# A scan, attention and expert kernel on one core: expert sums moved to SBUF, lane copies ahead of the exponentials, weighted sums behind the scores

## The chip, the cores and the metric

The kernel runs on one core of a Trainium2 chip. The metric is the device time of one execution in microseconds. The core has five engines with a queue each: TensorE (PE, whose weight loads are listed apart as PEld), VectorE (DVE), ScalarE (ACT), GpSimd (POOL) and SyncE (SP), which issues all the transfers that matter here. Each engine works its queue off in the order in which the program put it there.

## The reference

Two layers on an input of shape (4, 128, 64, 64): four images, 128 channels, 4096 positions each. All data are float32.

```
# layer 0
x = x + conv(group_norm(x))      # layer norm, depthwise 3x3, layer norm, gelu, 128x128, residual,
                                 # layer norm, then a selective scan on 4 chunks of 32 channels:
    h = dA_t * h + dBu_t         #   64 inner channels, 16 states each, over all 4096 positions
    y = einsum('bdn,bn->bd', h, C_t)
                                 # gate by silu(z), out_proj, skip, layer norm, proj_w
# layer 1, on tokens t (4, 4096, 128)
t = t + attention(layer_norm(t)) # 4 heads of 32, softmax(q k / sqrt(128)) v, W_proj
router_probs = softmax(n @ router_w + router_b)          # n = layer_norm(t), 8 experts
top_p, top_i = top_k(router_probs, 2); top_p = top_p / sum(top_p)
t = t + sum_k top_p[k] * (n @ expert_w[top_i[k]] + expert_b[top_i[k]])
```

## The kernel before

**Blocks, units, slots.** An image is cut into 8 blocks of 512 positions. A *unit* is one block, one half of the scan's channels (`p`) and one of the 16 states (`n`): 4 x 8 x 2 x 16 = 1024 units. The main loop (`while slot < len(units) ...`) runs in *slots*. Each slot does one unit of the scan: `fetched` brings the broadcast rows of B and C from DRAM (three slots ahead), `decayed` has ScalarE compute `da = exp(delta * a)` (one slot ahead), and `scan` gives VectorE three instructions of 128x512: `h = rows * du`, the scan itself, and `hc = rows * h`. ScalarE copies the last column of `h` into `states` at the top of the next slot. The sixteen `hc` of a block and half are added up by TensorE, as products with the identity into the bank `y`. For image 0 every `hc` goes to TensorE by itself; from image 1 on GpSimd first adds the even and the odd one (`even`), and TensorE gets half as many.

**Attention.** Beside the scan, each slot also does one *group* of attention once its quarter of the image is ready: `attention` is a generator that issues four matmuls of scores (`sc`, key side 128 rows, queries 512 columns, two banks at a time) and two exponentials (`pT`, 128x1024) on ScalarE. `weighted` issues the eight matmuls `av` of the group of the slot before; the two query blocks `u` use the two column halves of the array. When a part ends, `avs` is copied from PSUM, added to what an earlier part left (`prev`), and sent to DRAM. There are 1024 groups; attention of image b overlaps the scan of image b + 1, and the last image's attention has the core nearly to itself.

**Lanes.** Everything else is written as generators that are stepped in two *lanes*, X and Y, each with one PSUM bank (`work("X")`, `work("Y")`) and four temporaries. `advance(lane, second)` takes a lane one `yield` further. Each slot steps a lane twice: half A issues mostly TensorE work, half B mostly the VectorE, ScalarE or GpSimd work that reads it. Lane Y runs `group_norm`, `first_norm`, `conv` and `inputs` (in-projection, Silu, B and C, softplus); lane X runs `closed` (the end of layer 0, then keys, queries and values), `divided` (divides the attention sums) and `finished` (output projection, router, top-2, experts). `normalised` is the layer norm used in all of them: VectorE's statistics, four small GpSimd instructions (`rs`, `shift`), then four ScalarE instructions `xt`.

The order within a slot before is: transfers, `states` copy, `da`; scores and exponentials of this slot's group; X's half B if its last yield was `"short"`; scan; X's half B otherwise; Y's half A; `y` products that are due; Y's half B; `weighted` of the last group; X's half A. All queue orders follow from this, since the wrappers (`Queue`, line 445) record every instruction in program order; this is why the profile gives line 445 for nearly everything.

**Experts before.** In `finished`, for each of the 4 tiles of 128 tokens and each half of the experts, one matmul of 128x512 fills the X bank with four experts' outputs, tokens on partitions, and VectorE adds them to `acc` with four `scalar_tensor_tensor` of 128x128, weighted by `pr`. These 16 steps per block yield `"short"`, so that two fit in a slot. `divided` loads the four heads' sums (`avl`), transposes them, and multiplies by reciprocals; `finished` transposes the result back (`aT`).

**Transfers.** `send` collects stores, and `flush` issues them all at the top of the next slot on SP, ahead of the fetches of rows.

Of the kernel before, what the change touches and what calls it, by code (L numbers as in the profile page):

```python
# [17 lines left out]
P = 128  # L18
C = 128
# [17 lines left out]
def conv_mamba_attn_moe_kernel(ctx: ExitStack, tc: tile.TileContext, t: dict):  # L37
# [423 lines left out]
    def send(out, in_):  # L461
        outgoing.append((out, in_))

    def flush():
        for o, i in outgoing:
            sync.dma_start(out=o, in_=i)
        outgoing.clear()
# [32 lines left out]
    def normalised(lane, src):  # L500
# [15 lines left out]
        yield  # L516
# [9 lines left out]

    group_of, y0_of, xn_of, pairs_of, in_of, gated, kqv = {}, {}, {}, {}, {}, {}, {}
# [147 lines left out]
    def inputs(b, i, p):  # L675

        xn, pairs = xn_of[b, i], pairs_of[b, i]
        r = slice(DI * p, DI * p + DI)
        ps = work("Y")
# [15 lines left out]
        bc = mix.tile([DI, BLK], F32, name="bc")  # L695
        scalar.copy(bc, pb[0:DI, :])
        bcd = dram.tile([2, NST, 2 * BLK], F32, name="bcd", bufs=4)
        send(bcd.rearrange("c n (k q) -> (c n k) q", k=2), bc)
# [62 lines left out]
    def closed(b, i):  # L761
# [20 lines left out]
        summed(ps, [(wout[:, p, :], gated.pop((b, i, p))) for p in range(2)])  # L782
# [3 lines left out]
        yield  # L786
        ps = transposed("X", by_tile(cm))
        yield
        xt = yield from normalised("X", by_tile(ps))
        ps = transposed("X", xt)  # L790
        yield
# [9 lines left out]
        send(tsave[b][:, s], tt.rearrange("p j c -> p (j c)"))  # L801
# [4 lines left out]
        send(td[:, s], tr.rearrange("p j c -> p (j c)"))  # L806
        ps = transposed("X", xt)
        yield
# [3 lines left out]
        split = []  # L812
        for d, w, bias in ((kd, wkn, bkn), (qd, wqn, bqn)):
            ps = work("X")
            mm(ps, w, xa)
            yield
            full = side.tile([P, BLK], F32, name="full")
            scalar.activation(full, ps, AF.Identity, bias=bias)
            hi = side.tile([P, BLK], F32R, name="hi", bufs=2)
            scalar.activation(hi, ps, AF.Identity, bias=bias)  # L820
            yield

            split.append((d, full, hi))
            lower(split.pop(), sj)
# [9 lines left out]

    def lower(what, s):
        d, full, hi = what
        lo = side.tile([P, BLK], F32R, name="lo", bufs=2)
        vector.tensor_sub(lo, full, hi.bitcast(F32))
        for half, w in enumerate((hi, lo)):
            w = w.bitcast(F32)  # L840
            if len(d.shape) == 4:
                send(d[:, :, half, s], w[:, None, :].to_broadcast([P, 2, BLK]))
            else:
                send(d[:, half, s], w)
# [96 lines left out]
    sums, partial, ao_of = [None], {}, {}  # L941

    def weighted(group):
# [10 lines left out]
        if last:  # L954
# [5 lines left out]
            d = dram.tile([P, BLK], F32, name=f"avd{q}{h}")  # L960
            send(d, avs)
            partial[b, q, h] = d
            if final and h == NH - 1:
                lanes["X"].append((("div", b, q), divided(b, q), []))
                for u in range(2):
                    i = 2 * q + u
                    lanes["X"].append((
                        ("out", b, i), lambda lane, b=b, i=i: finished(b, i, lane),
                        [("div", b, q)],
                    ))  # L970

    def divided(b, q):

        ao = att.tile([P, 2, NT, NH, DH], F32, name="ao", bufs=2)
        ao_of[b, q] = ao

        def load(h):
            w = att.tile([P, BLK], F32, name="avl", bufs=2)
            sync.dma_start(out=w, in_=partial.pop((b, q, h)))
            return w  # L980

        ahead = load(0)
        yield
        yield
        for h in range(NH):
            now = ahead
            if h + 1 < NH:
                ahead = load(h + 1)
            ps = transposed("X", by_tile(now))
# [188 lines left out]
    while slot < len(units) or due or waiting or left or lanes["X"] or running:  # L1178
# [47 lines left out]
        if more:  # L1226
            advance("X", True)
# [117 lines left out]
```

## Time and profile before

| what | us |
|---|---|
| median of 3 runs (lowest, highest) | 5848.51 (5847.83, 5851.88) |
| the profiled execution | 5853.82 |
| its span, first to last instruction | 5852.1 |
| mean granted TensorE clock | 0.94 |

The first page of the profile gives each engine's busy time and groups instructions by what they write and read. A group's line has the count, the busy time, the mean of one in ns, and then the idle time of the engine just before these instructions with what ended it. A stretch's line has the time, then busy time and count of PE, PEld, DVE, ACT and (where it worked) POOL, the granted clock, the share of the 16 DMA engines in use, and GB/s. A line of waits says who waited for whose work: total us, times, longest. Matmuls overlap, and one of a group can show more time than it keeps the array.

### The profile page before, as it was taken

The numbers are of one execution on the slowest core, as the hardware profiler recorded it, in microseconds if no ns is written. First come the engines' busy times: TensorE is split into PE (matmuls) and PEld (weight loads), VectorE is DVE, ScalarE is ACT, GpSimd is POOL, SyncE is SP. The second block draws the span as 40 slices with busy tenths as digits, with TensorE's granted clock in tenths as the row PEclk, the third lists the DMA queues.
The fourth block names the chain that finished last, engine by engine and source line by source line (L and its number), as shares of the span: only waits on it lengthen the run. The fifth ranks groups of instructions, "written<-read, shape, count | busy, mean of one in ns | idle before, by whom it ended". The sixth has DMA issues, their size and how long they took to land. (4 is left out here: it accounts for less than half of the span.)

```text
span 5852.1 us, 61426 instructions
## 1 busy us (share of the span) xinstructions
PE 5075.6 (87%) x18378; PEld 2129.7 (36%) x18378; DVE 4221.9 (72%) x7155; ACT 3988.0 (68%) x6116; POOL 2033.6 (35%) x1821
## 2 busy tenths in 40 slices
PE   4676898988989898898999998898999998998896
PEld 2222343333333333333333333333333343343332
DVE  4888766778877787787888887888888888712222
ACT  3454676877767776777777776677877777665452
POOL 2333222335423443444443443444443434310000
PEclk8777999999999998999999999999999999999997
DMA  3455565556545555556555555457555555533211
GB/s 98 167 177 169 196 203 182 190 209 223 202 149 172 198 186 197 172 198 219 185 199 199 188 199 191 155 196 252 191 192 199 183 201 185 190 134 102 99 58 35
DMA packets 405509, 1030.33 MB, mean 176 GB/s; under 512 B 42785, under 2 KB 126130, under 8 KB 405170
## 3 DMA queue, kind: packets, MB, share of 16 engines
q1 hardware_dynamic: 404002, 1025.53, 51.5%
q8 instruction: 149, 2.44, 0.2%
q14 instruction: 190, 1.56, 0.1%
q10 hardware_dynamic: 1168, 0.80, 0.1%
HBM read 875.11 MB, written 134.22 MB: 172 GB/s over the span
## 5 line engine op out<-in xcount | busy, mean ns | idle before, releaser
L445 ACT ACTIVATE pT<-sc 128x1024 f32<-128x1024 f32 x2048 | 1981.1, 1020 | 879.0 <-PE sc L445 875.5
L445 PE MATMUL av<-pT,v 128*64 128x512 f32 x8192 | 2012.4, 612 | 0.5 <-ACT avs L445 0.2
L445 DVE TENSOR_TENSOR_SCAN h<-da,state,h 128x512 f32<-128x512 f32 x896 | 1271.6, 1419 | 276.2 <-ACT da L445 191.5
L445 PE MATMUL sc<-qs,ks 128*128 128x512 f32 x4096 | 1326.7, 445 | 76.7 <-ACT pT L445 40.3
L445 POOL TENSOR_TENSOR hc<-hc 128x512 f32<-128x512 f32 x384 | 557.4, 1452 | 1541.4 <-DVE hc L445 1367.3
L445 PEld LDWEIGHTS sc<-qs,ks 128*128 128x128 f32 x4096 | 724.5, 193 | 663.0 <-issue 240.9
L445 PEld LDWEIGHTS av<-pT,v 128*64 128x64 f32 x8192 | 503.9, 138 | 1198.3 <-issue 1115.1
L445 DVE TENSOR_TENSOR hc<-rows,h 128x512 f32<-128x512 f32 x1024 | 828.2, 809 | 73.6 <-DVE h L445 2.3
L445 DVE TENSOR_TENSOR h<-rows,du 128x512 f32<-128x512 f32 x1024 | 821.7, 802 | 57.3 <-DMA rows<-bcd 30.9
L445 PE MATMUL y<-hc,ident 128*128 128x512 f32 x1280 | 734.3, 660 | 79.6 <-DVE hc L445 70.0
L445 ACT ACTIVATE da<-delta,amat 128x512 f32<-128x512 f32 x1024 | 749.7, 732 | 30.9 <-DVE h L445 28.7
L445 ACT COPY state<-h 128x1 f32<-128x1 f32 x896 | 176.8, 197 | 373.3 <-DVE h L445 373.0
L445 DVE SCALAR_TENSOR_TENSOR acc<-ps_X,prX,acc 128x128 f32<-128x128 f32 x864 | 301.8, 349 | 169.6 <-PE ps_X L445 145.3
L445 ACT ACT_TABLE_LOAD x318 | 408.0, 1283 | 20.0 <-PE ps_Y L445 15.3
L445 PE MATMUL ps_X<-w_ew,xf 128*128 128x512 f32 x432 | 257.2, 679 | 112.4 <-DVE acc L445 112.2
L445 PEld LDWEIGHTS y<-hc,ident 128*128 128x128 f32 x1280 | 248.7, 206 | 257.1 <-DVE hc L445 129.6
L445 DVE RECIPROCAL rden<-ps_X 128x8 f32<-128x8 f32 x64 | 13.0, 203 | 348.8 <-PE ps_X L445 348.6
L445 POOL TENSOR_SCALAR rsX<-mvX 128x4 f32<-128x4 f32 x92 | 48.3, 525 | 600.6 <-DVE mvX L445 593.6
L445 POOL TENSOR_SCALAR du<-e 128x512 f32<-128x512 f32 x64 | 129.3, 2020 | 322.3 <-ACT e L445 322.3
L445 POOL TENSOR_TENSOR avs<-avs,prev 128x512 f32<-128x512 f32 x64 | 94.6, 1478 | 420.4 <-ACT avs L445 345.8
L445 POOL TENSOR_SCALAR rsY<-mvY 128x4 f32<-128x4 f32 x100 | 54.9, 549 | 533.6 <-DVE mvY L445 532.0
L445 ACT ACTIVATE xt<-ps_Y,shiftY,rsY 128x128 f32<-128x128 f32 x380 | 143.5, 467 | 127.4 <-POOL shiftY L445 119.9
(244 smaller groups left out, 5052.1 us busy)
## 6 DMA issues: line engine op xcount, KB each, us to landing
rows<-bcd SPq DMA_DIRECT2D x1024, 512.0 KB, 4.9
ks<-kd SPq DMA_DIRECT2D x256, 512.0 KB, 6.3
qs<-qd SPq DMA_DIRECT2D x130, 512.0 KB, 5.6
v<-vd SPq DMA_DIRECT2D x256, 256.0 KB, 6.2
avd<-avs SPq DMA_DIRECT2D x128, 256.0 KB, 2.0
pairs<-xn SPq DMA_DIRECT2D x128, 128.5 KB, 2.4
qd<-hi SPq DMA_DIRECT2D x32, 512.0 KB, 5.6
qd<-lo SPq DMA_DIRECT2D x32, 512.0 KB, 5.9
```

The source lines that it names most:

```text
L445: return lambda *args, **kw: queued(op(*args, **kw))
```

## The change

In words, in the order of the diff:

- `send` takes a number of slots, and `flush` holds a store back that long. Stores of B and C rows, `tt`, `tr` and the result wait 2 slots, attention sums 3.
- `held` keeps `inputs` and the first normalisation of `closed` from using the X bank at once.
- `"early"` replaces `"short"`: where a lane X generator yields it, its next half B (ScalarE copies and activations: `xt`, `f`, `xa`, `xf`, the router's exponential, `prT`, `res`) is issued ahead of this slot's scores and exponentials instead of behind the scan.
- The out-projection `wout` is issued as two matmuls with 64 output rows each, one per half.
- The low part `lo` of keys and queries is computed from PSUM by one VectorE instruction; ScalarE's `full` goes.
- `divided` goes. Final attention sums are stored to `total` with rows in the order of the heads; `inverted` loads the denominators as 128x32, takes reciprocals, stores `inverse`; `finished` loads the sums and the reciprocals and multiplies.
- The router's probabilities are no longer divided by their sum (the top-2 weights are normalised later anyway).
- Experts: the weights of the 8 experts go to DRAM (`shares`), come back broadcast over partitions two experts at a time (`share`), VectorE multiplies them into `xf` (128x1024), and two matmuls with the experts' weights as stationary operand give the sum of two experts, which VectorE adds to `res`.
- `weighted` of the last group is issued right behind this slot's scores.
- GpSimd's pairwise sums begin at slot 128 (`ALONE`) rather than at image 1 (slot 256).
- The order of lane Y's tasks at an image's start changes, and blocks wait for `freed` instead of `closed`.

```diff
-    def send(out, in_):
-        outgoing.append((out, in_))
+    def send(out, in_, slots=1):
+        outgoing.append([slots, out, in_])
     def flush():
+        for entry in outgoing:
+            entry[0] -= 1
+            if entry[0] == 0:
+                sync.dma_start(out=entry[1], in_=entry[2])
...
@@ normalised
         yield
-        yield
+        yield "early"
         xt = tmp(lane, "xt", [P, NT, C])
...
@@ inputs
+        while held:
+            yield
+            yield
+        held.add("in")
...
@@ closed
-        summed(ps, [(wout[:, p, :], gated.pop((b, i, p))) for p in range(2)])
+        for p in range(2):
+            r = slice(DI * p, DI * p + DI)
+            mm(ps[r, :], wout[:, p, r], gated.pop((b, i, p)))
+        done.add(("freed", b, i))
...
-            full = side.tile([P, BLK], F32, name="full")
-            scalar.activation(full, ps, AF.Identity, bias=bias)
             hi = side.tile([P, BLK], F32R, name="hi", bufs=2)
             scalar.activation(hi, ps, AF.Identity, bias=bias)
+            lo = side.tile([P, BLK], F32R, name="lo", bufs=2)
+            vector.scalar_tensor_tensor(
+                lo, ps, bias, hi.bitcast(F32), ALU.add, ALU.subtract
+            )
...
@@ weighted, after the last group of a head
+            d = total[b, q]
+            send(d[:, :, h].rearrange("u k r q -> (u k) r q"), avs, 3)
+            if h == NH - 1:
+                work_left = inverted(b, q)
+                later.extend((slot + n, work_left) for n in (4, 6, 8))
+
+    def inverted(b, q):
+        den = small.tile([P, 2 * NH * BLK // P], F32, name="den", bufs=1)
+        n = den.shape[1]
+        for u in range(2):
+            sync.dma_start(
+                out=den[DI * u : DI * u + DI, :],
+                in_=total[b, q][u, 1, :, 0].rearrange("h (a n) -> h a n", n=n),
+            )
+        yield
+        vector.reciprocal(den, den)
+        inverse[b, q] = d = dram.tile([2, NH, BLK], F32, name="inverse")
+        send(d.rearrange("u h (a n) -> (u h a) n", n=n), den)
+        yield
...
@@ finished
+        sync.dma_start(out=aT, in_=total[b, q][u, 0].rearrange("h d q -> (h d) q"))
+        sync.dma_start(
+            out=inv, in_=inverse[b, q][u][:, None, :].to_broadcast([NH, DH, BLK])
+        )
...
+        vector.tensor_mul(aT, aT, inv)
...
-        for j in range(NT):
-            for u in range(2):
-                ps = work(lane, [P, NE // 2, C])
-                mm(
-                    ps.rearrange("p e c -> p (e c)"), xf[:, j * P : (j + 1) * P],
-                    ewf[:, u * BLK : (u + 1) * BLK],
-                )
-                yield "short"
-                for e in range(NE // 2):
-                    k = NE // 2 * u + e
-                    vector.scalar_tensor_tensor(
-                        acc[:, j, :], ps[:, e, :], pr[:, j, k : k + 1], acc[:, j, :],
-                        ALU.mult, ALU.add,
-                    )
...
+        shares = dram.tile([NE, BLK], F32, name=f"shares{lane}")
+        send(shares, prT)
...
+        def share(e):
...
+            sync.dma_start(
+                out=w.rearrange("p k q -> p (k q)"),
+                in_=shares[e : e + 2].rearrange("e q -> (e q)")[None].to_broadcast([P, 2 * BLK]),
+            )
+            return w
...
+        ahead = deque(share(e) for e in (0, 2))
+        yield
+        yield
+        for e in range(0, NE, 2):
+            if e + 4 < NE:
+                ahead.append(share(e + 4))
+            yield
+            w = ahead.popleft()
+            if e:
+                vector.tensor_add(res, res, ps)
+            vector.tensor_mul(w, w, xf[:, None, :].to_broadcast([P, 2, BLK]))
+            yield
+            ps = work(lane)
+            for u in range(2):
+                mm(ps, ew[:, e + u, :], w[:, u, :], u == 0, u == 1)
...
@@ the main loop
+        taken = early["X"] and advance("X", True)
         group = next(groups, None)
-        taken = short["X"] and advance("X", True)
+        if waiting:
+            weighted(waiting)
+        waiting = group
         if slot < len(units):
...
-            if b == 0:
+            if slot < ALONE:
                 due.append((slot + 1, unit, hc, n == 0))
...
         advance("Y", True)
-        if more:
-            advance("X", True)
-        if waiting:
-            weighted(waiting)
-        waiting = group
         advance("X", False)
+        while later and later[0][0] <= slot:
+            next(later.popleft()[1])
         slot += 1
```

## The prediction

> **What bounds the kernel now.** I read the first page, then the stretches, then the waits inside the long stretch, then one slot in order of time. The page first: shares of the engines and the groups that the change touches (columns: count, busy us, mean ns of one, idle of the engine before it and who ended it).
>
> ```profile
> PE 5075.6 (87%) x18378; PEld 2129.7 (36%) x18378; DVE 4221.9 (72%) x7155; ACT 3988.0 (68%) x6116; POOL 2033.6 (35%) x1821
> ...
> L445 ACT ACTIVATE pT<-sc 128x1024 f32<-128x1024 f32 x2048 | 1981.1, 1020 | 879.0 <-PE sc L445 875.5
> L445 PE MATMUL av<-pT,v 128*64 128x512 f32 x8192 | 2012.4, 612 | 0.5 <-ACT avs L445 0.2
> ...
> L445 POOL TENSOR_TENSOR hc<-hc 128x512 f32<-128x512 f32 x384 | 557.4, 1452 | 1541.4 <-DVE hc L445 1367.3
> ...
> L445 DVE SCALAR_TENSOR_TENSOR acc<-ps_X,prX,acc 128x128 f32<-128x128 f32 x864 | 301.8, 349 | 169.6 <-PE ps_X L445 145.3
> ```
>
> No engine is full: TensorE leads, yet ScalarE waits 875 us for scores and VectorE 145 us for expert products. The table of stretches (busy us of each engine, granted clock, DMA share) separates the stages: scan alone, first attention, scan and attention, attention alone, the end.
>
> ```profile
> 100.00:600.00 500.00, 331.44 (x692) 125.74 (x692) 422.29 (x587) 255.31 (x495) 164.34 (x150) 0.75 0.50 168
> 600.00:1100.00 500.00, 459.99 (x1610) 190.88 (x1608) 346.49 (x499) 361.22 (x563) 140.65 (x131) 0.96 0.57 194
> 1100.00:5110.00 4010.00, 3600.61 (x13454) 1519.56 (x13454) 3252.50 (x5315) 2988.26 (x4587) 1663.86 (x1427) 0.96 0.57 194
> 5110.00:5750.00 640.00, 588.35 (x2384) 249.08 (x2386) 141.34 (x502) 350.70 (x416) 41.19 (x56) 0.99 0.28 94
> 5750.00:5852.00 102.00, 55.35 (x130) 25.43 (x126) 35.96 (x134) 8.89 (x19) 3.40 (x8) 0.57 0.06 22
> ```
>
> In the 4010 us that decide, TensorE is 90% busy, VectorE 81%, ScalarE 75%. Three in-order queues that near one another lose time by handing over, and the waits from 600 to 5110 us name the hand-overs.
>
> ```profile
> ACT pT L445 <- PE sc L445: 607.2, 470, 8.5
> DVE acc L445 <- PE ps_X L445: 134.3, 51, 5.5
> PE ps_X L445 <- DVE acc L445: 73.7, 65, 4.8
> PE ps_X L445 <- ACT xt L445: 56.5, 46, 4.9
> ACT xin L445 <- PE ps_Y L445: 49.8, 12, 9.1
> PE ps_X L445 <- DMA avl<-avd: 39.1, 13, 8.2
> DVE stY L445 <- PE ps_Y L445: 33.5, 25, 6.4
> ```
>
> VectorE and TensorE wait for each other over one expert bank. The next rows are one lane normalisation: its shift is ready on GpSimd, ScalarE does the two exponentials first, then xt, and TensorE's transposes (and the next scores behind them) wait.
>
> ```profile
> 3222.22 1.94 ACT L445 ACTIVATE pT<-sc 128x1024 f32<-128x1024 f32 x2 [1.21 <-PE sc L445]
> 3222.67 0.24 POOL L445 TENSOR_SCALAR shiftX<-shiftX 128x4 f32<-128x4 f32 x1
> 3224.05 1.51 ACT L445 ACTIVATE xt<-ps_X,shiftX,rsX 128x128 f32<-128x128 f32 x4
> 3225.61 0.66 PE L445 MATMUL ps_X<-ident,xt 128*128 128x128 f32 x4 [0.72 <-ACT xt L445]
> ```
>
> **What the Trainium skill says.** (1) "Perfetto Trace Analysis", section "Tensor Engine Instruction (MATMUL, LD_WEIGHTS)": ACT, DVE and GpSimd are strict FIFO and a matmul's end is modelled. The trace agrees: eight av, 0.6 us each, fill 1.94 us, so 90% busy is not full. (2) "SBUF — State Buffer", section "SBUF: two separate sides": a DVE instruction with two SBUF inputs and a GpSimd instruction lock each other out. Here hc took 0.69 us alone and 1.52 beside GpSimd. The removed expert updates read PSUM (349 ns, up to 354 at most), the new products read SBUF twice. (3) "VectorE: DVE Perf Modes", section "Mode 1× (REGULAR)": one result a cycle; it prices the new product below. (4) "TensorE: Matmul & The Clock Gate", section "Part 3: Packing small matmuls": column groups of the array work side by side. The av halves do so here.
>
> **The change part by part.** Counts are from the two built orders, which take 1205 slots before and 1203 after, with 1024 scan slots and 1024 attention groups in both; so the time per slot decides. "Mixed" is 600 to 5110 us.
>
> *Experts.* Out: 1024 updates on VectorE. In: 128 products of 128x1024 and 128 additions from PSUM; matmuls stay at 256 of 128x512. Mixed: 728 updates x 0.349 = 254 us, and 147 us of VectorE idle before them, 401 us for 22.75 blocks, 17.6 each. A product: 512 elements take 0.69 us, the page's cycle adds 512/0.96 = 0.53, so 1.22 (estimate); times 0.81/0.69 (mean of hc over hc alone) 1.43. Four are 5.7, four additions at 0.686 (row tt from ps_X) 2.7, and 0.5 us wait each, 2: 10.4. So 7.2 x 22.75 = 164 us of VectorE's time, plus 3 softmax steps of 0.2 to 0.4 us a block, 17. VectorE is 80% busy and its relief partly meets the other queues: I take 110 of 181; bounds 0 and 181.
> Their cover: each pair of shares goes through DRAM. The write lands in about 2 us, the read of 512 KB like rows<-bcd in 4.9, fetched two slots (some 10 us) ahead. Without that cover VectorE would stand before the product with the next scan behind it; 128 x 2 us = 256. The 64 MB are 6% more traffic on DMA at 57%, so I take 0. The share reads join SP's one queue ahead of rows fetches; a blocked one delays rows, which are three slots ahead.
>
> *Division.* Out: per two blocks 4 x (0.203 + 0.424) on VectorE, 24 transposes on TensorE, the avl waits (39 us). In: a product of 0.7 per block, a reciprocal, two DRAM round trips started 4 to 8 slots after the sums. Net -30; bounds 0 and -75.
>
> *ScalarE.* 56 "full" x 0.70 and 23 aT x 0.59 go: 53 us. It idles 607 us for scores, so -25; bounds 0 and -53. The new lo reads PSUM at about the same 0.7.
>
> *Even lanes.* For slots 128 to 255, 64 y products of two matmuls go: 0.95 us from start to start, 61 us on a TensorE that is 92% busy from 600 to 1100. GpSimd gains 64 x 1.45 = 93 us at 28% busy and may lock VectorE (69%). -35; bounds -61 and +30.
>
> *wout* in 64-column halves, side by side: 32 x 0.8 = 26 us of TensorE, -12; bounds 0 and -26.
>
> *Early copies.* f, xa, xf, the router's exponential, prT and res (some 150 in the mixed stage) go ahead of 1.94 us of exponentials. TensorE's idle for exactly these is 36 us by group. Queued behind each are the exponentials, so the next scores: 0.2 to 0.6 us. xt (78): in the slot shown the shift is ready at 3222.91, so xt would end at 3224.4 instead of 3225.6, but the exponentials start 2.2 us later; the next scores, which had to wait for the transposes until 3226.0, can start at about 3225.4, and the exponentials after them no earlier. A wash. Net 0; bounds -93 (36 and xt's 56) and +170 (78 x 2.2).
>
> *Weighted sums behind the scores.* The eight av hold TensorE 1.87 us and pass the Y lane and y. Less: waits of ps_Y and y products, 18 + 29 + 19 + 11 = 77 us by group. More: ScalarE in the 108 input stages (Silu; Abs, Exp, Ln) waits for matmuls now behind av. There the exponentials (about 1.8 us past the scores) cover most of 1.87 but not the 0.9 to 2.6 us of matmuls: up to 1.4 x 108 = 150. Freed earlier by res, the X bank gives some back (12.6 us before w_wbc). Net 0; bounds -77 and +150.
>
> *Attention alone*, 640 us: VectorE is 22% busy and hides the products; the experts' bank wait goes (136.5 us in all, less 73.7 mixed and about 35 in the end: 28) and divisions: -35. *End*, 102 us: experts alternate bank by bank from 5785 to 5841, 56 us; two blocks x 8 matmul pairs x 2.05 at half clock are 33, plus about 6 on VectorE: -17. Division -5, two more DRAM bounces at 3.3 us +7: -15. The scan-only head keeps its work: 0. *Delayed sends* cost nothing, as their readers are 4 slots or more later.
>
> Sum: -110 - 30 - 25 - 35 - 12 + 0 + 0 - 35 - 15 = -262. The profiled execution took 5853.8, its span 5852.1; the median of the runs is 5848.5. 5848.5 - 262 = 5587, taken as 5590.
>
> **The rivals.**
> *ScalarE late, slower.* xt stands in front of the exponentials until GpSimd is done, and input matmuls stand behind av. All 78 x 2.2 + 150 = 322 us come through: 5848 - 262 + 322 = 5908. It decides once four fifths of that lateness reaches the end. For: the slot shown; ScalarE's chain in input stages. Against: TensorE's waits at the same places shrink.
> *Relief without effect.* VectorE and ScalarE get work off, but slots stay set by hand-overs; only y, wout, attention alone and the end pay: 97 us, 5751. For: three engines share the stage.
> *Hand-overs come free.* All 93 + 77 us of TensorE's lane waits go as well: 5590 - 170 = 5420. For: ScalarE's 607 us. Against: bounds of both edits have two signs.
>
> **How the numbers follow.** About 0.2% (12 us) is what a measurement can tell from no change. Forecast 0.49 (its own range 5500 to 5690), relief without effect 0.20, hand-overs free 0.11, cancelled within 12 us 0.03, slower 0.17. Faster is 0.49 + 0.20 + 0.11 = 0.80. The range from 5420 to 5880 leaves out half of the freest case and about 0.1 of the slower one.
>
> **What would show it.** Right: in the mixed stage VectorE's wait for expert products falls from 134 us to under 40, share products near 1.4 us, the slot with experts no longer above its neighbours; attention alone about 600 us; the end under 95. Wrong: a new wait of xt for shiftX above 150 us, xin and e waiting for ps_Y above 150, products near 2 us beside GpSimd, or VectorE waiting for share by DMA.

## The result: slower by 1%

| | us |
|---|---|
| before, median of 4 runs (lowest, highest) | 5849.78 (5847.83, 5851.88) |
| after, median of 4 runs (lowest, highest) | 5907.88 (5903.34, 5919.31) |
| after / before, with 95% interval | 1.0102 (1.0085 to 1.0120) |
| span of the profiled execution, before and after | 5852.1, 5901.6 |
| mean granted TensorE clock, before and after | 0.940, 0.922 |

The forecast was 5590, and the range ended at 5880. The change costs 58 us instead of saving 260.

The first page of the kernel after: shares of the engines, then groups (count, busy us, mean ns of one, idle of the engine before it and who ended most of it).

```profile
PE 5080.1 (86%) x17866; PEld 2069.8 (35%) x17866; DVE 4123.8 (70%) x6211; ACT 3932.9 (67%) x6020; POOL 2141.3 (36%) x1885
...
L445 ACT ACTIVATE pT<-sc 128x1024 f32<-128x1024 f32 x2048 | 1983.3, 1023 | 820.1 <-PE sc L445 818.1
L445 PE MATMUL av<-pT,v 128*64 128x512 f32 x8192 | 2090.9, 633 | 0.0
...
L445 POOL TENSOR_TENSOR hc<-hc 128x512 f32<-128x512 f32 x448 | 663.2, 1481 | 1651.5 <-DVE hc L445 1479.8
...
L445 DVE TENSOR_TENSOR share<-share,xf 128x1024 f32<-128x1024 f32 x128 | 174.4, 1363 | 43.3 <-DMA share<-sharesY 30.3
```

VectorE has 98 us less to do than before (4123.8 against 4221.9), ScalarE 55 us less (3932.9 against 3988.0), TensorE 512 matmuls less. The work that was to go is gone; the time is not. The table of stretches after (busy us of PE, PEld, DVE, ACT, POOL, granted clock, DMA share, GB/s) shows it in the long stretch.

```profile
100.00:600.00 500.00, 329.23 (x684) 124.37 (x682) 421.61 (x585) 249.94 (x481) 164.61 (x151) 0.75 0.50 168
600.00:1100.00 500.00, 439.12 (x1514) 177.71 (x1516) 375.69 (x501) 362.72 (x567) 218.27 (x185) 0.92 0.58 195
1100.00:5110.00 4010.00, 3547.89 (x12752) 1445.09 (x12749) 3068.37 (x4520) 2857.34 (x4405) 1647.73 (x1404) 0.94 0.60 200
5110.00:5750.00 640.00, 607.33 (x2387) 253.43 (x2385) 208.84 (x412) 381.49 (x463) 88.15 (x89) 0.98 0.47 155
5750.00:5852.00 102.00, 81.71 (x330) 32.45 (x328) 1.72 (x4) 51.57 (x54) 0.00 (x0) 0.91 0.18 54
```

From 1100 to 5110 us every one of the three engines is less busy than before (PE 3548 against 3601, VectorE 3068 against 3252, ScalarE 2857 against 2988), and the clock is 0.94 against 0.96. Three engines wait more, so something makes them wait for one another. The fourth row is busier than before only because the scan now runs on into it.

Stretches at fixed times mix stages once the kernels drift apart, so from here on I cut each trace at the first and the last of its own scans (VectorE's `h <- da, state, h`) and at the last exponentials. In us:

| stage | before | after | difference | predicted |
|---|---|---|---|---|
| slots 0 to 127, scan only | 577.6 | 579.3 | +2 | 0 |
| slots 128 to 255, even lanes new | 602.8 | 602.4 | 0 | -35 |
| slots 256 to 1022, all together | 3937.0 | 4084.6 | +148 | -177 |
| attention alone | 630.8 | 560.3 | -70 | -35 |
| end | 103.9 | 75.0 | -29 | -15 |

(The 177 are experts 110, division 30, ScalarE 25 and `wout` 12.) The two last stages give twice what was predicted, in part because work moved ahead of them: by the last scan 24 of the 32 blocks of experts are done, 23 before. The stages with a scan in every slot lose what they were to gain. These are the waits of the kernel after from 600 to 5000 us, a stretch that lies inside the scan in all the kernels (who waited for whom: total us, times, longest).

```profile
ACT pT L445 <- PE sc L445: 563.3, 361, 6.5
DVE h L445 <- ACT da L445: 340.3, 118, 8.4
...
ACT xt L445 <- POOL shiftX L445: 186.4, 58, 5.6
...
PE sc L445 <- ACT pT L445: 153.3, 189, 3.4
...
ACT xt L445 <- POOL shiftY L445: 119.7, 63, 4.6
DVE stY L445 <- PE ps_Y L445: 102.2, 50, 7.5
...
DVE xin L445 <- PE y L445: 92.6, 34, 5.4
```

The same waits before:

```profile
DVE h L445 <- ACT da L445: 196.8, 76, 21.5
...
ACT xt L445 <- POOL shiftY L445: 46.9, 32, 4.5
...
PE sc L445 <- ACT pT L445: 40.3, 63, 4.6
...
ACT xt L445 <- POOL shiftX L445: 37.6, 18, 5.6
DVE xin L445 <- PE y L445: 37.0, 20, 4.5
...
DVE stY L445 <- PE ps_Y L445: 33.5, 25, 6.4
```

Two families have grown: ScalarE at `xt` of lane X, which is an early copy, and everything that follows lane Y's matmuls. The scan's own wait, `h` for `da`, grew most, by 143.5 us; the runs below divide it up. Two places in order of time (start, duration, engine, operation, in brackets the idle time before it and who ended it) show one of each. First lane Y:

```profile
3278.95 1.94 PE L445 MATMUL av<-pT,v 128*64 128x512 f32 x8
...
3280.82 0.66 PE L445 MATMUL ps_Y<-ident,gn 128*128 128x128 f32 x4
...
3281.51 0.89 DVE L445 BATCH_NORM_STATS2 stY<-ps_Y 128x6 f32<-128x128 f32 x4 [1.95 <-PE ps_Y L445]
...
3282.77 0.57 POOL L445 TENSOR_SCALAR rsY<-mvY 128x4 f32<-128x4 f32 x1 [8.14 <-DVE mvY L445]
...
3286.76 1.51 ACT L445 ACTIVATE xt<-ps_Y,shiftY,rsY 128x128 f32<-128x128 f32 x4 [2.79 <-POOL shiftY L445]
```

The transposes into `ps_Y` start when the eight `av` ahead of them have gone in, 1.87 us after these started. VectorE, whose next instruction reads `ps_Y`, stands for 1.95 us; everything from the statistics to `xt` is late by as much, and ScalarE then stands for 2.79. Next lane X:

```profile
3300.66 1.12 PE L445 MATMUL y<-hc,ident 128*128 128x512 f32 x2
...
3303.25 0.24 POOL L445 TENSOR_SCALAR shiftX<-shiftX 128x4 f32<-128x4 f32 x1
...
3303.52 1.51 ACT L445 ACTIVATE xt<-ps_X,shiftX,rsX 128x128 f32<-128x128 f32 x4 [4.73 <-POOL shiftX L445]
...
3304.91 1.95 ACT L445 ACTIVATE pT<-sc 128x1024 f32<-128x1024 f32 x2
3305.08 1.11 PE L445 MATMUL ps_X<-ident,xt 128*128 128x128 f32 x4 [3.30 <-ACT xt L445]
3306.00 2.13 PE L445 MATMUL sc<-qs,ks 128*128 128x512 f32 x4
```

ScalarE stands 4.73 us for GpSimd with the exponentials queued behind `xt`. TensorE gets nothing for 3.30 us, and its next four scores take 2.13 us, where four took 1.17 at 3281.23. The next eight `av` take 3.46 us instead of 1.94. That is the half clock: the trace's clock record is at 0.5 from 3304.35 to 3311.17. The Trainium skill ("TensorE: Matmul & The Clock Gate", section "Part 1: The HAM clock gate (the "warmup" mystery)") says that the array drops to half rate after an idle window of about 3.4 us. Here the record drops when TensorE, by the modelled end of its last matmul, has been idle for 2.6 us; the last section counts such spells. Between 600 us and the last scan the clock records of before show 325 us at the lower level, those of after 567.

### The profile page after: what moved, and what is told of

Read it like the earlier page. It is cut to its first block, busy times and chain, and to the rows that moved or that the text cites. A ratio compares the mean times of both kernels' runs of the same rounds, so it can differ in the third digit from the quotient of the medians.

```text
span 5901.6 us, 59661 instructions
## 1 busy us (share of the span) xinstructions
PE 5080.1 (86%) x17866; PEld 2069.8 (35%) x17866; DVE 4123.8 (70%) x6211; ACT 3932.9 (67%) x6020; POOL 2141.3 (36%) x1885
## 4 chain that ended last, share of the span: by engine, by line
PE 36%; DVE 22%; ACT 14%; POOL 5%; issue 3%; DMA 3%; SPq 0%; DVEq 0%; ACTq 0%; POOLq 0%
PE av L445 15%; DVE h L445 10%; PE sc L445 9%; PE ps_X L445 6%; ACT pT L445 4%; PE ps_Y L445 3%; DVE hc L445 3%; ACT L445 3%; DVE cm L445 3%; PE y L445 3%; POOL rsX L445 2%; ACT xt L445 2%; DMA inv<-inverse 2%; DVE share L445 1%; ACT da L445 1%
## 5 line engine op out<-in xcount | busy, mean ns | idle before, releaser
L445 PE MATMUL av<-pT,v 128*64 128x512 f32 x8192 | 2090.9, 633 | 0.0
L445 PE MATMUL sc<-qs,ks 128*128 128x512 f32 x4096 | 1444.5, 472 | 189.5 <-ACT pT L445 159.8
L445 POOL TENSOR_TENSOR hc<-hc 128x512 f32<-128x512 f32 x448 | 663.2, 1481 | 1651.5 <-DVE hc L445 1479.8
L445 DVE TENSOR_TENSOR h<-rows,du 128x512 f32<-128x512 f32 x1024 | 847.8, 828 | 42.8 <-POOL du L445 29.3
L445 PE MATMUL y<-hc,ident 128*128 128x512 f32 x1152 | 687.2, 683 | 68.5 <-DVE hc L445 64.9
L445 ACT ACT_TABLE_LOAD x318 | 408.0, 1283 | 80.1 <-PE ps_Y L445 75.8
L445 PEld LDWEIGHTS y<-hc,ident 128*128 128x128 f32 x1152 | 197.9, 206 | 468.0 <-issue 221.0
L445 ACT ACTIVATE xt<-ps_Y,shiftY,rsY 128x128 f32<-128x128 f32 x380 | 143.5, 462 | 203.5 <-POOL shiftY L445 192.7
L445 PE MATMUL ps_X<-share,w_ew 128*128 128x512 f32 x448 | 221.1, 616 | 26.6 <-DVE share L445 21.3
L445 DVE TENSOR_TENSOR_SCAN h<-da,h 128x512 f32<-128x512 f32 x128 | 176.2, 1376 | 62.1 <-ACT da L445 52.0
L445 DVE TENSOR_TENSOR share<-share,xf 128x1024 f32<-128x1024 f32 x128 | 174.4, 1363 | 43.3 <-DMA share<-sharesY 30.3
L445 PE MATMUL ps_X<-ident,xt 128*128 128x128 f32 x372 | 91.8, 332 | 130.5 <-ACT xt L445 100.4
```

The source lines that it names most:

```text
L445: return lambda *args, **kw: queued(op(*args, **kw))
```

## The experiments

Four accounts were open: the weighted sums stand at the wrong place; the early copies do; ScalarE's and VectorE's new low part `lo` is late; or the planned savings were never there. All ratios are to the kernel before, with 95% intervals; sizes are differences of medians. The medians of the kernel before, taken beside each of them, lie between 5849.8 and 5858.9 us, so a difference between two runs that were not made together can be off by some 10 us.

### The two moves undone, apart and together

`weighted` back at its old place, between lane Y's half B and lane X's half A:

```diff
         group = next(groups, None)
-        if waiting:
-            weighted(waiting)
-        waiting = group
...
         advance("Y", True)
+        if waiting:
+            weighted(waiting)
+        waiting = group
         advance("X", False)
```

> The changed kernel with the weighted sums back at their old place, behind lane Y and the y products; early copies stay. Theory A: 5908 falls by 100 to 200 us, to 5710 to 5810, and VectorE's wait of stY for TensorE (126 us) and of xin for y (115 us) go back to about 55 and 50. Theory E: within 40 us of 5908. Theory X: within 40 us of 5908.

No early copies; all of lane X's half B stand behind the scan:

```diff
-        taken = early["X"] and advance("X", True)
+        taken = False
```

> The changed kernel with all of lane X's half B behind the scan again (no early copies); the rest of the change stays. Theory E (xt in front of the exponentials keeps ScalarE waiting for GpSimd's shift): 5908 falls by 100 to 200 us, to 5710 to 5810, and ScalarE's wait of xt for shiftX falls from 222 to under 80 us. Theory A (the loss comes from the weighted sums behind the scores): within 40 us of 5908. Theory X (the experts' and the division's own transfers and products cost the time in the mixed stage): within 40 us of 5908.

Both edits:

> The changed kernel without early copies and with the weighted sums at their old place: experts in SBUF, division through DRAM, ScalarE's and TensorE's removals alone. The prediction's sum without its two zero terms was -262 us: 5590 to 5700 if theories E and A together hold the loss. Theory X: still 5850 or more.

Only the four `xt` of lane X's normalisation late, the other copies still early:

```diff
@@ normalised
-        yield "early"
+        yield
```

> The changed kernel with the normalisation's xt behind the scan again, while the copies f, xa, xf, prT, res and the router's exponential stay early. Theory E in its narrow form (it is GpSimd's shift that is late): all of the gain of the run without any early copies, or more, 5700 to 5810. If instead any work ahead of the exponentials costs its own length: about half of that gain.

| kernel | us | ratio | against after |
|---|---|---|---|
| after | 5907.88 | 1.0102 (1.0085 to 1.0120) | |
| `weighted` at its old place | 5718.15 | 0.9768 (0.9752 to 0.9784) | -190 |
| no early copies | 5873.54 | 1.0032 (1.0020 to 1.0045) | -34 |
| neither | 5708.39 | 0.9749 (0.9732 to 0.9765) | -199 |
| only `xt` late | 5837.60 | 0.9972 (0.9962 to 0.9981) | -70 |

The place of eight matmuls is worth 190 us, more than the whole loss; without it the change is faster by 2.3%, as theory A had it. Theory E's 100 to 200 us for the early copies did not come. The early copies are two things of opposite sign: with `xt` taken out the others gain (5837.6 against 5873.5 without any, 36 us), and `xt` costs 70. The same waits, 600 to 5000 us, with `weighted` at its old place:

```profile
ACT pT L445 <- PE sc L445: 594.9, 402, 8.1
DVE h L445 <- ACT da L445: 277.4, 115, 7.6
...
ACT xt L445 <- POOL shiftX L445: 210.8, 58, 6.8
...
PE sc L445 <- ACT pT L445: 71.7, 156, 3.0
...
ACT xt L445 <- POOL shiftY L445: 41.9, 38, 3.9
...
DVE stY L445 <- PE ps_Y L445: 36.9, 29, 5.5
...
DVE xin L445 <- PE y L445: 29.4, 22, 3.1
```

The lane Y family is back where it was before the change: `shiftY` 119.7 to 41.9, `stY` 102.2 to 36.9, `xin` 92.6 to 29.4. The table load ahead of Silu, which waits for `ps_Y`, went from 56.0 to 13.4. That is 249 us of waits less on VectorE and ScalarE, and `h` waits 63 us less for `da`, for 190 us of time. `xt` for `shiftX` is still there at 210.8: it belongs to the early copies, not to the place of `weighted`.

### Which hand-over does the place hurt?

Lane Y's half A ahead of `av`, the `y` products still behind it:

```diff
         advance("Y", False)
+        if waiting:
+            weighted(waiting)
+        waiting = group
         while due and due[0][0] <= slot:
```

> The changed kernel with the weighted sums behind lane Y's half A but ahead of the y products (and of Y's half B). If the loss is lane Y's half A being late for the VectorE and ScalarE work of half B: 5720 to 5760, nearly all of the 190 us back. If it is the y products being late (xin waits for y 115 us, 65 more than before): little back, 5860 or more.

The other way round, the `y` products ahead of `av` and lane Y's half A behind it:

```diff
-        advance("Y", False)
         while due and due[0][0] <= slot:
...
+        if waiting:
+            weighted(waiting)
+        waiting = group
+        advance("Y", False)
         advance("Y", True)
```

> The changed kernel with the y products ahead of the weighted sums and lane Y's half A behind both. The counterpart of the run with lane Y's half A ahead: theory of the late half A: 5860 or more; theory of the late y products: 5720 to 5790.

`weighted` at its old place only in the 251 slots in which lane Y is in `inputs`, the stage that the prediction had priced:

```diff
-        if waiting:
-            weighted(waiting)
-        waiting = group
+        behind = slot in INPUT_SLOTS
+        if not behind:
+            if waiting:
+                weighted(waiting)
+            waiting = group
...
         advance("Y", True)
+        if behind:
+            if waiting:
+                weighted(waiting)
+            waiting = group
         advance("X", False)
```

> The changed kernel; the weighted sums stand behind lane Y and y only in the 251 slots in which lane Y runs inputs, and right behind the scores in all others. Moving them everywhere gave back 190 us (5908 to 5718). Theory I (ScalarE's Silu and softplus chains of the input stages, which wait for the matmuls now behind av, carry the loss): at least two thirds of it, 5720 to 5780. Theory N (VectorE's statistics and the y products, in all other slots, carry it): less than a third, 5845 or more.

`lo` as before the change, from ScalarE's `full` and in the half step after, with `weighted` at its old place:

```diff
+            full = side.tile([P, BLK], F32, name="full")
+            scalar.activation(full, ps, AF.Identity, bias=bias)
...
-            vector.scalar_tensor_tensor(
-                lo, ps, bias, hi.bitcast(F32), ALU.add, ALU.subtract
-            )
...
+            split.append((d, full, hi))
+            lower(split.pop(), sj)
...
+    def lower(what, s):
+        d, full, hi = what
+        lo = side.tile([P, BLK], F32R, name="lo", bufs=2)
+        vector.tensor_sub(lo, full, hi.bitcast(F32))
```

> From the run with the weighted sums back at their old place (5718): lo again as a difference of two SBUF tiles, issued one half later, with ScalarE's full back in. Theory L: the new lo, issued in the same half as hi, makes VectorE (and the next scan behind it) wait for ScalarE (lo for hi 184 us against 88 before) and holds the X bank longer: 5718 falls by 40 to 80 us although ScalarE gets 45 us more work. If the wait is idle time of VectorE that costs nothing: 5718 rises by 0 to 25 us.

| kernel | us | ratio | gained |
|---|---|---|---|
| lane Y's half A ahead of `av` | 5791.93 | 0.9893 (0.9877 to 0.9910) | 116 of 190 |
| `y` products ahead of `av` | 5865.56 | 1.0013 (1.0005 to 1.0021) | 42 of 190 |
| old place in the `inputs` slots | 5819.86 | 0.9932 (0.9913 to 0.9951) | 88 of 190 |
| old place everywhere, old `lo` | 5723.19 | 0.9774 (0.9757 to 0.9790) | +5 on 5718.15 |

Both hand-overs count, lane Y's half A most; the first and the third run lie between their two expectations. In the second run half A also stands behind the `y` products (1.12 us a pair), so 42 is not their share alone; the remaining 32 us (21 by the ratios) are not much more than the noise. The old place in the `inputs` slots gives back 88 us; the rest lies in the other slots or needs both. The form of `lo` costs nothing: with the old form the time is the same within the intervals. What `lo`'s wait for `hi` costs stays open, as the old form waits nearly as long (154.8 us against 165.5; 80.1 in the kernel before).

### The place alone, and the other savings alone

The kernel before, with nothing changed but `weighted` right behind the scores:

```diff
         group = next(groups, None)
+        if waiting:
+            weighted(waiting)
+        waiting = group
         taken = short["X"] and advance("X", True)
...
-        if waiting:
-            weighted(waiting)
-        waiting = group
         advance("X", False)
```

> The kernel before with one edit alone: the weighted sums right behind the scores. If their place is what made the changed kernel slower, and not their meeting with its other edits, 5849 rises by 120 to 200 us, to 5970 to 6050. If the loss needs the changed kernel's early copies or experts: within 40 us of 5849.

6052.73, ratio 1.0331 (1.0314 to 1.0348): 197 us above the kernel before beside it (5855.73). So the loss is the move's own, and does not need the new experts, the early copies or anything else of the change. What moves with the eight `av` are ScalarE's copy `avs` and GpSimd's addition to it, at a part's end; no run moves them apart. Its waits show the same family (600 to 5000 us):

```profile
DVE stY L445 <- PE ps_Y L445: 108.8, 52, 8.4
ACT xt L445 <- POOL shiftY L445: 107.8, 58, 5.2
...
DVE xin L445 <- PE y L445: 78.8, 30, 6.4
...
ACT L445 <- PE ps_Y L445: 52.1, 26, 2.7
```

The next three start from the version with `weighted` at its old place (5718.15). The old experts, one matmul and its four updates a slot, so that neither the trips through DRAM nor the products are there:

```diff
+        for j in range(NT):
+            for u in range(2):
+                ps = work(lane, [P, NE // 2, C])
...
+                yield
+                for e in range(NE // 2):
+                    k = NE // 2 * u + e
+                    vector.scalar_tensor_tensor(
+                        acc[:, j, :], ps[:, e, :], pr[:, j, k : k + 1], acc[:, j, :],
+                        ALU.mult, ALU.add,
+                    )
+                yield
...
-        shares = dram.tile([NE, BLK], F32, name=f"shares{lane}")
-        send(shares, prT)
...
-            vector.tensor_mul(w, w, xf[:, None, :].to_broadcast([P, 2, BLK]))
-            yield
-            ps = work(lane)
-            for u in range(2):
-                mm(ps, ew[:, e + u, :], w[:, u, :], u == 0, u == 1)
```

> From the run with the weighted sums at their old place (5718): the old experts (matmuls with tokens as stationary side, 32 updates of 128x128 from PSUM per block, two half steps a slot, without the two-in-a-slot pacing of before); division, lanes, lo and wout stay changed. The prediction's term for the experts was 110 us in the mixed stage plus some 45 in attention alone and the end: 5718 rises by 120 to 180 us. If the experts' relief went into hand-overs, as the traces suggest for the mixed stage (3937 us before and 3924 in the run with both order edits undone, for slots 256 to 1022): a rise of 60 us or less, nearly all after the last scan.

Even lanes from slot 256 again:

```diff
-    ALONE = NB // 2 * 2 * NST
+    ALONE = NB * 2 * NST
```

> From the run with the weighted sums at their old place (5718): GpSimd's pairwise sums begin with image 1 again (slot 256 in place of 128). The prediction's term was 35 us; the traces show 27 us for slots 128 to 255: 5718 rises by 20 to 40 us. If GpSimd's lock on VectorE ate the gain: within 10 us.

And the version that the first four runs point to, `weighted` at its old place, plain copies early, `xt` late:

```diff
@@ normalised
-        yield "early"
+        yield
```

> The changed kernel with the weighted sums at their old place and the normalisation's xt behind the scan, the plain copies early. The run without any early copies took 5708 and the one with all of them 5718. If plain copies ahead of the exponentials are worth something by themselves: 5660 to 5700. If they are worth nothing: 5700 to 5715.

| kernel | us | ratio | against 5718.15 |
|---|---|---|---|
| old experts | 5755.54 | 0.9827 (0.9811 to 0.9844) | +37 |
| even lanes from slot 256 | 5748.36 | 0.9812 (0.9795 to 0.9828) | +30 |
| `xt` late | 5663.62 | 0.9675 (0.9659 to 0.9692) | -55 |

The new experts are worth 37 us, not the 155 that the prediction had for them in all stages (of the 181 us behind its 110, 17 were for three steps of the softmax, which stay out in this run). By stage (us):

| stage | old experts | new experts |
|---|---|---|
| slots 128 to 255 | 578.2 | 576.5 |
| slots 256 to 1022 | 3925.1 | 3927.7 |
| attention alone | 593.6 | 550.6 |
| end | 79.9 | 76.0 |

Where three engines share the stage, its time is the same. The stages are not quite alike, though: by the last scan the old form has done 716 of its 1024 updates, 22.4 blocks of 32, the new one 24, and at slot 960 the new form is 16 us ahead of the old, counted from slot 256. So the new experts are worth little there rather than nothing, and some of the 43 us in attention alone is work that they had already done. The two-in-a-slot pacing of before, which this run lacks, may also account for some of it. Busy time of the old and then of the new from 600 to 5080 us (PE, PEld, DVE, ACT, POOL, clock, DMA share, GB/s):

```profile
600.00:5080.00 4480.00, 3977.99 (x14592) 1650.12 (x14592) 3608.09 (x5677) 3292.18 (x5067) 1896.98 (x1621) 0.96 0.59 196
```

```profile
600.00:5080.00 4480.00, 4020.87 (x14775) 1669.54 (x14775) 3578.82 (x5180) 3306.67 (x5096) 1942.95 (x1625) 0.96 0.62 207
```

497 instructions of VectorE are gone, but only 29 us of its busy time, and GpSimd is 46 us busier with practically the same number of instructions. VectorE's waits for the bank went (for `ps_X` before `acc`, 97.4 to 9.3 us) and others came from 600 to 5000 us: `res` for `ps_X` 0 to 43.1, `h` for `da` 213.3 to 277.4, `lo` for `hi` 131.3 to 165.5. In these four groups it waits 53 us more (43.1 + 64.1 + 34.2 - 88.1).

Even lanes: from 600 to 1150 us without them (first) and with them (second):

```profile
600.00:1150.00 550.00, 521.32 (x1844) 215.35 (x1844) 395.73 (x569) 413.71 (x632) 159.89 (x150) 0.97 0.60 201
```

```profile
600.00:1150.00 550.00, 493.35 (x1760) 200.91 (x1762) 436.31 (x579) 418.83 (x638) 248.77 (x208) 0.95 0.61 205
```

TensorE falls from 95% to 90% busy, and VectorE and ScalarE get a little more done. In the profiled executions, 8.5 us of the gain lie in slots 128 to 255 (585.0 against 576.5) and 28 in the slots after (3956.1 against 3927.7), where nothing was edited; what brings these was not found.

`xt` late gives the fastest kernel, 3.3% below the one before. Its waits from 600 to 5000 us:

```profile
ACT pT L445 <- PE sc L445: 684.7, 459, 8.0
...
ACT xt L445 <- POOL shiftX L445: 65.5, 39, 5.6
...
PE ps_X L445 <- ACT xt L445: 83.0, 48, 6.9
```

`xt` for `shiftX` fell from 210.8 to 65.5 us. TensorE's wait for `xt` rose by 12 (71.3 to 83.0), the price that the early place was meant to save. ScalarE's idle for scores rose by 90, and the kernel is faster all the same.

### Would it be faster still if av came last of all?

If every matmul that another engine waits for should go ahead of `av`, lane X's half A should as well. From the fastest version:

```diff
         advance("Y", True)
+        advance("X", False)
         if waiting:
             weighted(waiting)
         waiting = group
-        advance("X", False)
```

> The fastest run so far (5664), with the weighted sums one place further back, behind lane X's half A too, last of all in the slot. Theory H (lane matmuls pay for whatever TensorE does ahead of them, because ScalarE and VectorE wait for them, while nobody waits for the weighted sums): lane X's half A gains as lane Y's did: 5664 falls by 20 to 80 us. Theory B (the old place is a balance: matmuls of lane X that are issued sooner only wait for their own inputs on TensorE, without the weighted sums to cover the wait): 5664 rises by 20 us or more.

And the counterpart of the `inputs` slots, the old place in all the slots but those:

```diff
-        behind = slot in INPUT_SLOTS
+        behind = slot not in INPUT_SLOTS
```

> The counterpart of the run in which the weighted sums stood behind lane Y in input slots alone (5820, 88 of the 190 us back): here they stand behind lane Y and y in all slots but those. If what a slot costs is its own hand-overs, the two parts add up: 100 us back, 5790 to 5825. If one late slot makes its neighbours late (the whole gain needs both): less than 60 back, 5850 or more.

`av` last of all: 6058.40, ratio 1.0352 (1.0331 to 1.0374), 395 us above the fastest version. Waits from 600 to 5000 us:

```profile
ACT pT L445 <- PE sc L445: 983.5, 521, 8.7
...
PE ps_X L445 <- ACT xt L445: 152.4, 64, 6.9
ACT avs L445 <- PE av L445: 138.1, 72, 6.8
...
PE ps_X L445 <- DVE lo L445: 118.0, 49, 4.5
```

TensorE now waits for what lane X's half A reads, which VectorE and ScalarE make in the same slot (`xt` 83.0 to 152.4, `lo` 51.9 to 118.0), and `av` is no longer there to fill that time but stands in front of the next scores (ScalarE 684.7 to 983.5). So `av` is a filler, and of the places tried one is good: behind the matmuls that others wait for in this slot (lane Y, `y`), ahead of those that wait for others (lane X).

The counterpart: 5844.76, ratio 0.9978 (0.9970 to 0.9985), 63 us below after. With the 88 of the `inputs` slots this makes 151 of 190. The other 39 us (23 by the ratios) come only with both sets. So the `inputs` slots hold 88 us if they are put right first and 127 if last, the others 63 to 102.

The waits of the changed kernel and its five versions with another place for `av` (total us from 600 to 5000):

| wait | right behind the scores | half A ahead | `y` ahead | old place in `inputs` slots | old place in the others | old place |
|---|---|---|---|---|---|---|
| `stY` for `ps_Y` | 102.2 | 29.4 | 112.6 | 98.1 | 30.0 | 36.9 |
| `xt` for `shiftY` | 119.7 | 67.2 | 106.5 | 117.9 | 39.0 | 41.9 |
| `xin` for `y` | 92.6 | 111.0 | 30.1 | 85.0 | 37.6 | 29.4 |
| Silu's table load for `ps_Y` | 56.0 | 11.9 | 79.1 | 17.4 | 63.1 | 13.4 |
| `h` for `da` | 340.3 | 286.1 | 386.1 | 244.0 | 371.8 | 277.4 |
| time gained | | 116 | 42 | 88 | 63 | 190 |

In the first four rows each move takes away the waits of what it brings forward, and no others. But waits are not time. The other slots put right take 208 us off the first three rows and bring 63 us; the `inputs` slots put right leave these rows nearly as they were, take 39 us off the table load and 96 off the scan's wait for `da`, and bring 88. This fits a ScalarE that is late in the `inputs` stage and hands its lateness to VectorE's scan; no run shows that apart. GpSimd's wait for `avs`, which also grew with the move (114 us at the old place, 236 after), does not explain the late `shiftY`: with the old place in the other slots it is still 178, and `xt` waits 39.0.

## Why the prediction was wrong

**Weighted sums behind the scores, "Net 0; bounds -77 and +150".** This is the step that failed: it measured +190 in the new kernel and +197 in the old one, outside its own upper bound. The mechanism was in the working (matmuls behind `av`, 1.87 us late, with another engine waiting), and it failed in two ways. It was priced in the `inputs` stages alone, with up to 150 us: these measured 88 to 127. What was left out is the other engines' steps behind lane Y's matmuls and `y`, VectorE at `stY`, ScalarE at `xt` behind `shiftY` and VectorE at `xin` behind `y`: 206 us of new waits in the two profiles above (77.8 + 65.3 + 63.2), for 63 to 102 us of time. And it was put at zero because TensorE's own lane waits would shrink in return. They did, those at `ps_Y` and `y` from 106 us at the old place to 42, but TensorE then waited for the exponentials instead (`sc` for `pT`, 71.7 to 153.3).

**Early copies, "Net 0", "A wash" for `xt`.** Net is +34 in the change as made, +10 (inside the intervals) with `weighted` at its old place, but not because nothing happens: `xt` costs 55 to 70, the others save 36 to 45. The slot that the prediction showed had its shift ready at 3222.91, 1.1 us before `xt` started, and in that it was not typical: after the change `xt` finds its shift missing 58 times from 600 to 5000 us. The sign of the danger was named ("xt for shiftX above 150 us") and came, 186 us from 600 to 5000. A price of 2.2 us for each of 78 (172) was too high, zero was too low.

**Experts, -110 in the mixed stage.** Measured from 0 at the last scan to some 16 at slot 960. More than half of the 181 us behind it was idle time of VectorE (147 us before the old updates, less the 2 us a block given to the new form), counted as if an idle that ends is a gain; it did end (88 us less), and 141 us came in front of other instructions. Of busy time, 254 us were to become some 190, a relief of 63, and it was 29. The product itself was priced right, 1.43 us against 1.363. In attention alone and the end, 45 were predicted and 47 measured (43.0 + 3.9), of which some is the work moved ahead.

**Even lanes, -35.** Measured -30, but the agreement is partly luck: the term was for slots 128 to 255, and only 8.5 us fell there in the profiled executions.

**ScalarE -25, division -30, `wout` -12.** Only `lo` from PSUM, which takes 56 `full` off ScalarE (39 of the 53 us behind the -25), was measured alone: 5 us, within the intervals. With both moves undone the kernel differs from the one before by its savings alone, and slots 256 to 1022 then take 3924.2 against 3937.0: 13 us, where these three and the experts were to bring 177. These 13 hide two signs: slots 256 to 511 gain 43 us and 512 to 767 gain 12, but 768 to 1022 lose 42 (1258.1 before, 1300.4). Put back the old experts or the old `lo`, and these last slots still take 1289.0 and 1305.6, so what slows them is another part of the change, such as the division, `wout`, lane Y's new order, the delayed stores or the pacing of the experts that went; no run tells which. Of the division the waits show that it changed hands: TensorE's 37.7 us for `avl` went (600 to 5000 us), and VectorE now waits 37.2 at `aT` for `inv` from DRAM.

**Attention alone -35, end -15.** Measured -80 and -28 with `weighted` at its old place. Experts account for 47 of these 108; the other 61 are from the division, `wout`, the order of lane Y, the delayed stores or the block of work that now lies ahead of the last scan, and no run tells these apart.

**The rivals.** The sum of "ScalarE late, slower" gave 5908, which is the time measured, but that is luck, as its parts are not: 172 for `xt` were some 70, 150 for `av` were 190, the plain copies at 0 gained 36, and the savings of 262 were 146 (ratio 0.9749 with both moves undone). "Relief without effect" is nearly what the savings did in the mixed stage. That two rivals would come true together was given no chance.

**The signs named.** Right ones that came: products near 1.4 us, attention alone near 600 (560), the end under 95 (75.0), and, just, VectorE's wait for the sums of experts, 39.3 in the mixed stage with under 40 named. One did not come: slots with experts still stand above the others (6.17 us against 5.21 on average in slots 256 to 1021; 6.32 and 4.82 before). Of the wrong ones, `xt` for `shiftX` came; `xin` and `e` for `ps_Y` did not (18.0 and 14.3 us from 600 to 5000, and 56.0 at the table load ahead of Silu, with 150 named): most of lane Y's lateness was awaited elsewhere.

**The clock.** The prediction counted it in the end stage alone. With `weighted` at its old place the time at the lower level falls from 567 to 372 us between 600 us and the last scan. As work there took up to nearly twice as long (2.13 against 1.17 us, 3.46 against 1.94), at most half of these 195 us, some 100 of the 190, is an estimate of what passes through the clock; how much of it lies on the path was not shown apart.

By the runs, the loss divides into savings -146, early copies +10 and place of the weighted sums +190, together +54. These add up by construction, since each step starts where the one before it ends; what is left to the measured +58 lies between the two medians of the kernel before (5854.36 and 5849.78).

## What to carry to other kernels

Among the matmuls of one queue, place work that nobody awaits soon, such as `av` here, behind those whose readers stand in the same slot and ahead of those whose inputs are still being made: from the fastest kernel, 5664 us, moving it ahead of the first cost 174 us and behind the second 395. Pull a small instruction ahead of a long one only if all that it reads is ready by then; check its slowest producer over all its places, not in one slot. Where several engines hand over to one another within each slot, busy time and idle time taken off one engine are no gain until the wait that follows next has been named. And compare stages only when as much work lies in each: a faster version pulls work across the border.

## What was not expected of the hardware

Waits of 2 to 5 us in a TensorE that is about 90% busy go with hundreds of microseconds at half clock: 325 us in the kernel before, 567 after and 320 in the fastest version, each between 600 us and the last scan. The Trainium skill (same page, section "HAM oscillation — how this bites in real kernels") describes this for a kernel that waits for transfers; here it comes from waits between engines, as in the 3.30 us ahead of the transposes above, and moves with the order of the instructions. It does not take the page's 3.4 us: of TensorE's idle spells of 2 to 3.4 us (by the modelled ends of matmuls), 31 of 42 before, 69 of 77 after and 39 of 49 in the fastest version met a drop to half clock while they lasted or within 6.8 us. Of the spells of 0.5 to 1.5 us only 11 of 162, 31 of 134 and 16 of 148 did, about as many as chance would give (13, 23 and 14% of stretches of 9 us taken at random).
